# A four-layer sequence kernel: sums issued two pairs late, larger rings, background steps that end their slot, and some norms' statistics on ScalarE

## The chip, the cores and the metric

The kernel runs on one core of a Trainium2 chip. The metric is the device time of one execution in microseconds, given as the median of several runs. All data are float32.

## What is computed

`x` has two batches of 1024 positions with 256 features. Four layers follow each other, each conditioned on a vector of 512 values per batch, and each adds its result to its input.

```python
# layer 0: a selective scan
xn = layernorm(x, g, b) * (1 + scale) + shift          # shift, scale, gate from silu(c)
x_in, z = split(xn @ in_proj)                           # 2 x 512 channels
u = silu(causal_conv4(x_in) + conv_b)
dt_r, B, C = split(u @ x_proj)                          # 64, 16, 16
dt = softplus(dt_r @ dt_proj + dt_b)
h[t] = exp(dt[t] * A) * h[t-1] + (dt[t] * u[t]) * B[t]  # 512 channels x 16 states
y = sum_n(h[t] * C[t]) + u * D
x = x + gate * ((y * silu(z)) @ out_proj)
# layer 1: norm, affine (= skip), norm, then two such scans of one projection, forward and
#          backward in time; both multiplied by silu(mx), added, projected; plus skip
# layer 2: attention with softmax over features (q) and positions (k): k^T v first, then q
# layer 3: ordinary attention, 16 heads of 16, softmax over 1024 positions
```

Layers 2 and 3 end with a norm of the result, an affine, a silu, a projection and the addition to `x`.

## The kernel before

**The scans.** There are six scan passes: layer 0 for batch 0 and 1, then layer 1 forward and backward for batch 0, and the same for batch 1. A pass has 64 tiles of 128 rows by 1024 positions, where the rows are 32 channels by 4 states. Each tile takes five steps. ScalarE makes the decay `dA` in PSUM from `sp0`, the spread `dt` (`decay`, line 133). GpSimd makes the input from `sp1` and the row tile `bc[0]` (`inputs`, line 936). VectorE runs the recurrence (`tile`, lines 943 and 947). The product with `bc[1]` is made on VectorE (line 950), or, for some tiles, on GpSimd (line 949). TensorE adds up the states with the `fold` matrix (`fold`, line 974) into a bank `ys`, after `begin` has put `u * D` there (lines 960 and 964). Four pairs of tiles fill one bank, and `finish` (line 982) multiplies it by the gate and stores it.

**The order.** `chain` writes the order out by hand, pair by pair. Within pair `p` it issues inputs up to tile `2p+4` and decays up to `2p+2`, so that these run ahead. A running figure `lead`, kept from `spent["DVE"]` and the work given to GpSimd, decides which tile's product goes to GpSimd. The sums of pair `p-1` are issued at the end of pair `p`. The tile that an input fills lives until its sums are done; there are 8 such tiles (`hbp`). Decays alternate between two PSUM tiles.

**The work behind the scans.** All other work (norms, projections, conditioning, layers 2 and 3 of batch 0) is written as generators whose steps stand in a queue, `Behind`. Twice a pair, `slot` runs steps as long as there is credit, counted in TensorE columns (`RATES` per slot, at most `2 * T` saved), and room on ScalarE and GpSimd. Each engine executes its instructions in the order written. DMAs are issued from the SP queue, also in order; `later` and `save` put a DMA off by some slots, and `until` forces steps where something must be ready.

**Norms.** `normed` runs `stats` (VectorE, two rows for each 256 columns, lines 394 and 395), `root` (ScalarE, Ln and Exp), `refine` (one Newton step: seven small rows on GpSimd during the scans, lines 410 to 416, else four on VectorE) and `scaled` (eight ScalarE rows, line 133, or VectorE in the last stage). The scan stage holds eight norms.

**Lead-in.** Before the first tile, batch 0 passes through layer 0's norm, affine (`affine`), transposes (`channels`), projection, convolution and `ssm_inputs`. Then the first `sp` and `bc` tiles are loaded.

**Attention.** After the scans, `attention` runs layer 3's scores (line 1418), maxima (1427), exponentials and sums (1458), with layer 2 of batch 1 between them.

## Time and profile before

| | |
|---|---|
| median of 3 runs | 2124.39 us (2119.06 to 2125.03) |
| profiled execution | 2117.43 us, its span 2115.4 us |
| VectorE busy | 1745.5 us, 83% of the span |
| GpSimd busy | 1356.9 us, 64% |
| TensorE busy | 1626.8 us, 77% |
| ScalarE busy | 1140.4 us, 54% |
| DMA queue | 266.07 MB, 37.1% of 16 engines |

In the profile, PE is TensorE, DVE is VectorE, ACT is ScalarE, POOL is GpSimd and SP issues the DMAs. A row of the windows view gives a stretch, its length, the busy time of each engine in it with the number of its instructions, the granted TensorE clock as a share of full speed, the share of the DMA engines' time, and GB/s. A row of the waits view gives who waited for whom, the microseconds in total, the number of times, and the longest. A row of the timeline gives start, duration, engine, line, operation, output and input, and in brackets the idle time before it with what ended it.

### The profile page before, as it was taken

The page shows a single profiled execution, that of the slowest core. Times are in us where ns is not written, and L with a number is a line of the kernel's source. Part 1 is how long each engine was busy: PE and PEld are TensorE (multiplying, and loading weights), DVE is VectorE, ACT ScalarE, POOL GpSimd, SP SyncE. Part 2 cuts the span into 40 slices and gives each one's busy share as a digit, 9 for nine tenths or more (in the row PEclk, how much of TensorE's full clock was granted, in tenths as well). Part 3 has the DMA queues.
Part 4 walks back from the last instruction along what each step waited for, and adds up shares of the span by engine and source line. Part 5 has one row for each costly group of instructions (what it writes and reads, how often), then busy time and mean ns, then how long its engine had stood idle before and what let it go on. Part 6 is the DMA issues. An engine that isn't in the chain of part 4 may idle for free.

```text
span 2115.4 us, 22775 instructions
## 1 busy us (share of the span) xinstructions
PE 1626.8 (77%) x8112; PEld 617.7 (29%) x8112; DVE 1745.5 (83%) x1728; ACT 1140.4 (54%) x1583; POOL 1356.9 (64%) x667
## 2 busy tenths in 40 slices
PE   6576867288697547886945658944999899999997
PEld 3132313033141202222312323300545333333333
DVE  4688898898999999998999987998767757777763
ACT  5565666375546345764555453542044555656665
POOL 0789898898999999999998977998101211000000
PEclk9688968599796558988977865965899999999999
DMA  3663458245653555555653344332300111020001
GB/s 111 239 222 114 157 184 292 83 157 185 254 196 141 179 172 187 189 179 188 250 206 110 117 159 144 123 132 73 116 1 1 39 21 18 23 56 1 2 1 38
DMA packets 106870, 267.53 MB, mean 126 GB/s; under 512 B 14618, under 2 KB 39067, under 8 KB 106756
## 3 DMA queue, kind: packets, MB, share of 16 engines
q1 hardware_dynamic: 106756, 266.07, 37.1%
q8 instruction: 64, 1.05, 0.2%
q14 instruction: 50, 0.41, 0.1%
HBM read 195.90 MB, written 67.90 MB: 125 GB/s over the span
## 4 chain that ended last, share of the span: by engine, by line
PE 30%; DVE 10%; POOL 5%; issue 4%; ACT 2%; DMA 0%; DVEq 0%; ACTq 0%; POOLq 0%
PE sc_t L1418 13%; PE av_t L1458 6%; PE sc_t L95 4%; POOL hb_t L936 3%; PE bank_t L95 3%; DVE dA_t L943 2%; DVE mh L1427 2%; PE sc_t L99 2%; DVE dA_t L947 2%; POOL hb_t L949 1%; PE ys_t L974 1%; DVE hb_t L943 1%; ACT act_t L133 1%; POOL act_t L141 1%; DVE hb_t L947 1%
## 5 line engine op out<-in xcount | busy, mean ns | idle before, releaser
L936 POOL TENSOR_TENSOR hb_t<-sp,bc 128x1024 f32<-128x1024 f32 x384 | 908.8, 2399 | 88.5 <-PE ys_t L974 52.0
L133 ACT ACTIVATE dA_t<-sp,negA 128x1024 f32<-128x1024 f32 x384 | 428.5, 1117 | 548.3 <-DVE hb_t L950 432.8
L947 DVE TENSOR_TENSOR_SCAN dA_t<-dA_t,hb_t 128x1024 f32<-128x1024 f32 x195 | 445.9, 2287 | 62.3 <-ACT dA_t L133 35.1
L1427 DVE TENSOR_REDUCE mh<-sc_t 128x1 f32<-128x512 f32 x512 | 327.5, 686 | 110.2 <-PE sc_t L1418 109.8
L974 PE MATMUL ys_t<-hb_t,fold 128*32 128x512 f32 x1536 | 294.2, 781 | 153.5 <-POOL hb_t L949 101.1
L133 ACT ACTIVATE hb_t<-sc_t 128x512 f32<-128x512 f32 x512 | 276.9, 595 | 188.7 <-PE sc_t L1418 188.5
L950 DVE TENSOR_TENSOR hb_t<-dA_t,bc 128x1024 f32<-128x1024 f32 x285 | 349.1, 1225 | 21.4 <-DVE dA_t L947 0.5
L1418 PE MATMUL sc_t<-act_t 32*128 32x512 f32 x2048 | 336.6, 650 | 11.0 <-DVE mh L1427 7.3
L949 POOL TENSOR_TENSOR hb_t<-hb_t,bc 128x1024 f32<-128x1024 f32 x99 | 235.7, 2381 | 19.6 <-DVE hb_t L947 17.8
L784 POOL TENSOR_TENSOR act_t<-act_t,row 128x1024 f32<-128x1024 f32 x8 | 18.7, 2347 | 339.9 <-PE sc_t L99 193.3
L943 DVE TENSOR_TENSOR_SCAN dA_t<-dA_t,hb_t 128x1024 f32<-128x1024 f32 x90 | 205.7, 2285 | 9.2 <-POOL hb_t L936 6.0
L1458 PE MATMUL av_t<-hb_t,act_t 128*32 128x256 f32 x2048 | 164.3, 393 | 1.1 <-DVE act_t L1466 1.1
L95 PE MATMUL bank_t<-act_t,w_c_w 128*128 128x512 f32 x256 | 129.6, 657 | 41.2 <-ACT act_t L133 41.2
L133 ACT ACTIVATE act_t<-bank_t,cols 128x512 f32<-128x512 f32 (+1 forms) x206 | 129.9, 677 | 44.5 <-PE bank_t L95 38.7
L1418 PEld LDWEIGHTS sc_t<-act_t 32*128 32x128 f32 x2048 | 111.1, 185 | 120.9 <-issue 79.9
L974 PEld LDWEIGHTS ys_t<-hb_t,fold 128*32 128x32 f32 x1536 | 40.5, 123 | 358.9 <-POOL hb_t L949 139.5
L947 DVE TENSOR_TENSOR_SCAN hb_t<-dA_t,hb_t 128x1024 f32<-128x1024 f32 x61 | 139.0, 2279 | 3.9 <-ACT dA_t L133 3.6
L141 POOL TENSOR_TENSOR act_t<-act_t 128x1024 f32<-128x1024 f32 x50 | 118.4, 2367 | 0.2
L99 PE MATMUL bank_t<-ident,act_t 128*128 128x128 f32 x128 | 34.6, 426 | 92.5 <-ACT act_t L133 92.3
L95 PE MATMUL bank_t<-act_t,w_dt_w 64*128 64x512 f32 x96 | 74.6, 912 | 40.4 <-ACT act_t L133 34.4
L1458 PEld LDWEIGHTS av_t<-hb_t,act_t 128*32 128x32 f32 x2048 | 42.1, 108 | 190.5 <-issue 177.8
L1363 POOL MEMSET act_t<- 128x1024 f32 x8 | 7.6, 952 | 128.0 <-PE sc_t L1418 128.0
(176 smaller groups left out, 1833.9 us busy)
## 6 DMA issues: line engine op xcount, KB each, us to landing
sp<-dt SPq DMA_DIRECT2D x192, 512.0 KB, 5.3
dt<-act_t SPq DMA_DIRECT2D x48, 512.0 KB, 5.2
bc<-bc SPq DMA_DIRECT2D x48, 512.0 KB, 7.7
u<-act_t SPq DMA_DIRECT2D x24, 512.0 KB, 5.0
fu<-u SPq DMA_DIRECT2D x24, 512.0 KB, 4.5
y<-y SPq DMA_DIRECT2D x96, 128.0 KB, 5.8
g<-act_t SPq DMA_DIRECT2D x16, 512.0 KB, 5.3
fg<-g SPq DMA_DIRECT2D x64, 128.0 KB, 4.7
```

The source lines that it names most:

```text
L95: nc.tensor.matmul(o, w, x, **kw)
L133: nc.scalar.activation(o, x, func, **kw)
L141: nc.gpsimd.tensor_tensor(o, x, y, op)
L936: nc.gpsimd.tensor_tensor(e, self.sp[c, 1], self.bc[0][k], ALU.mult)
L943: nc.vector.tensor_tensor_scan(h[:, ::-1], dA[:, ::-1], e[:, ::-1], 0.0, ALU.mult, ALU.add)
L947: nc.vector.tensor_tensor_scan(h, dA, e, 0.0, ALU.mult, ALU.add)
L949: return lambda: nc.gpsimd.tensor_tensor(e, h, self.bc[1][k], ALU.mult)
L950: nc.vector.tensor_tensor(e, h, self.bc[1][k], ALU.mult)
L974: nc.tensor.matmul(self.ys[d, cp][at : at + DS, :], fold, e[:, ts(ch, 512)], start=False, stop=(k == NK - 1),)
L1418: nc.tensor.matmul(ps, w[r, ts(at, P)], x[r, ts(wide_at, 512)], start=True, stop=True)
L1427: nc.vector.tensor_reduce(mh[n][:, t, ch, j : j + 1], ps, AX.X, ALU.max)
L1458: nc.tensor.matmul(sums.av[32 * j : 32 * j + 32, ts(part, 256)], sts[b]["v"][t // 2][:, t % 2, 4 * g + j, :], es[j // 2][:, at : at + 256] ...
```

## The change

- The sums of pair `p-2` are issued at the end of pair `p`, and there are 9 input tiles instead of 8.
- `sp0` has four buffers instead of three and is loaded a step earlier. `bc` has a ring of four for each of its two kinds instead of one of eight, and the first kind is loaded ahead of a pair's slots. `u` and `y` for `begin` are loaded in halves, one for each bank.
- A step may yield `REST`: the slot then ends. Roots, refinements and the exponentials of layer 2 do so. The credit cap is `4 * T`, and three rates are higher.
- `refine` is always on VectorE. Statistics are made by `moments` on ScalarE (mean and sum of squares by the accumulator) for the norms that come while `mode["easy"]` is set: layer 1 of batch 1, and layers 2 and 3 of batch 0.
- In the lead-in, half of `scaled`, the affine, half of the transposes' evictions, both copies of `dbl` and the first input run on VectorE, and the first `bc` tile is loaded as soon as it is stored.
- `cond_later` runs once for each batch, the second time before `cond_last`, and loads its weights each time.
- Some small tiles move to other pools.

```diff
-RATES = (2048, 2048, 1250, 1300, 1500, 1500)
+RATES = (2048, 2600, 1500, 1500, 1500, 1500)
...
+REST = -1
...
     act = ctx.enter_context(tc.tile_pool(name="act", bufs=15))
-    hbp = ctx.enter_context(tc.tile_pool(name="hbp", bufs=8))
+    hbp = ctx.enter_context(tc.tile_pool(name="hbp", bufs=9))
...
-    mode = {"bank": "bank", "scans": False, "tail": False, "least": 640}
+    mode = {"bank": "bank", "scans": False, "tail": False, "least": 640, "easy": False}
...
             at = mod[:, scale_at + c, :]
+            if not mode["scans"]:
+                t = small_t((P, B), "aff")
+                nc.vector.tensor_scalar(t, at, 1.0, None, ALU.add)
+                nc.vector.tensor_scalar(s[:, c, :], t, g_c, None, ALU.mult)
+                nc.vector.scalar_tensor_tensor(
+                    o[:, c, :], t, b_c, mod[:, shift_at + c, :], ALU.mult, ALU.add
+                )
+                continue
...
-    def cond_later():
+    def cond_later(b):
...
         nc.sync.dma_start(g1[:, 1, :], a["norm1_b"].partition_broadcast(P))
-        yield 5 * T
+        yield 7 * T
...
         yield from pipe(*(
-            cond_rows(w, scb, brow, i * D, b, f"{name}1_{b}", res)
-            for b in range(B)
-            for i, (name, res) in enumerate(
-                (("shift", made), ("scale", made), ("gate", cond["gate1"]))
-            )
+            cond_rows(w, scb, brow, i * D, b, name, res)
+            for i, (name, res) in enumerate((
+                ("shift1", made), ("scale1", made),
+                ("gate1" if b == 0 else "gate0_0", cond["gate1"]),
+            ))
         ))
...
-    def root(mv):
+    def moments(src, mv):
+        for j in range(0, 4, 2):
+            for k in (j, j + 1):
+                act_f(
+                    small_t((P, 2, D), "t2", 1)[:, 0, :], src[:, k, :], AF.Identity,
+                    scale=-1.0 / D, accum_out=mv[:, k, 0:1],
+                )
+            for k in (j, j + 1):
+                act_f(
+                    small_t((P, 2, D), "t2", 1)[:, 0, :], src[:, k, :], AF.Square,
+                    bias=mv[:, k, 0:1], accum_out=mv[:, k, 1:2],
+                )
+            spent["ACT"] += 4 * 250
+            yield 320
+    def root(mv, easy):
         r = small_t((P, mv.shape[1]), "rstd", 2)
-        act_f(r, mv[:, :, 1], AF.Ln, bias=eps)
+        act_f(r, mv[:, :, 1], AF.Ln, bias=eps, scale=1.0 / D if easy else 1.0)
...
-    def refine(mv, r):
+    def refine(mv, r, easy):
         q = small_t((P, mv.shape[1]), "newt", 2)
-        e = nc.gpsimd if mode["scans"] else nc.vector
-        if mode["scans"]:
-            e.tensor_scalar(q, mv[:, :, 1], EPS, None, ALU.add)
-            e.tensor_tensor(q, q, r, ALU.mult)
-            e.tensor_tensor(q, q, r, ALU.mult)
-            e.tensor_scalar(q, q, -0.5, 1.5, ALU.mult, ALU.add)
-            e.tensor_tensor(r, r, q, ALU.mult)
-            e.tensor_scalar(q, mv[:, :, 0], -1.0, None, ALU.mult)
-            e.tensor_tensor(q, q, r, ALU.mult)
-            spent["POOL"] += 900
-            return q
-        e.scalar_tensor_tensor(q, mv[:, :, 1], EPS, r, ALU.add, ALU.mult)
-        e.scalar_tensor_tensor(q, q, -0.5, r, ALU.mult, ALU.mult)
-        e.scalar_tensor_tensor(r, q, 1.5, r, ALU.add, ALU.mult)
-        e.scalar_tensor_tensor(q, mv[:, :, 0], -1.0, r, ALU.mult, ALU.mult)
+        if easy:
+            nc.vector.tensor_scalar(q, mv[:, :, 1], 1.0 / D, EPS, ALU.mult, ALU.add)
+            nc.vector.tensor_tensor(q, q, r, ALU.mult)
+        else:
+            nc.vector.scalar_tensor_tensor(q, mv[:, :, 1], EPS, r, ALU.add, ALU.mult)
+        nc.vector.scalar_tensor_tensor(q, q, -0.5, r, ALU.mult, ALU.mult)
+        nc.vector.scalar_tensor_tensor(r, q, 1.5, r, ALU.add, ALU.mult)
+        nc.vector.scalar_tensor_tensor(
+            q, mv[:, :, 0], 1.0 if easy else -1.0, r, ALU.mult, ALU.mult
+        )
+        spent["DVE"] += 600
...
-    def scaled(src, r, q):
+    def scaled(src, r, q, i):
         o = abuf((P, 4, D))
-        for j in range(4 if mode["tail"] else 0):
+        far = mode["tail"] or i and not mode["scans"]
+        for j in range(4 if far else 0):
...
             )
-        for j in range(0 if mode["tail"] else 4):
+        for j in range(0 if far else 4):
...
         for i, t in enumerate(src):
-            stats(t, mv[:, ts(i, 4), :])
-            yield
-        r = root(mv)
-        yield mode["least"] * 3 // 2
-        q = refine(mv, r)
-        yield
+            if easy:
+                yield from moments(t, mv[:, ts(i, 4), :])
+            else:
+                stats(t, mv[:, ts(i, 4), :])
+                yield
+        r = root(mv, easy)
+        yield REST
+        q = refine(mv, r, easy)
+        yield REST
         for i, t in enumerate(src):
-            res.append(scaled(t, r[:, ts(i, 4)], q[:, ts(i, 4)]))
+            res.append(scaled(t, r[:, ts(i, 4)], q[:, ts(i, 4)], i))
...
         def take(i, c, ps):
+            if c and not (mode["scans"] or mode["tail"]):
+                nc.vector.tensor_scalar(
+                    dst[c][:, ts(i, 512)], ps, scale(c), bias(c), ALU.mult, ALU.add
+                )
+                return
...
                     )
-            take(0, pss[0])
-            nc.vector.tensor_copy(dbl[:, 512:], pss[1][: R + 2 * N, :])
+            for ch in range(2):
+                nc.vector.tensor_copy(dbl[:, ts(ch, 512)], pss[ch][: R + 2 * N, :])
...
         save(2, st["bc"], dbl[R : R + 2 * N, :])
+        if "first" in st:
+            later(2, st["first"])
...
             yield from normed(xt, skip)
+            yield REST
...
                 nc.vector.tensor_tensor(v, v, twice(cond["s1"][b], 4), ALU.mult)
+                spent["DVE"] += 1800
...
                 yield
+            yield REST
+            yield REST
...
                     least = next(self.queue[0])
+                    if least == REST and not mode["tail"]:
+                        self.credit -= max(work[0] - at, mode["least"])
+                        return 0
...
                 return
-            self.credit = min(self.credit + columns, 2 * T)
+            self.credit = min(self.credit + columns, 4 * T)
...
-        def load_bc(self, k):
-            for w in range(2):
-                t = bcp.tile([P, T], F32, tag="bc", name="bc")
-                at = w * N + k * NS
-                nc.sync.dma_start(
-                    t,
-                    self.st["bc"][at : at + NS, :].unsqueeze(0).to_broadcast([DS, NS, T]),
-                )
-                self.bc[w][k] = t
+        def load_bc(self, k, w):
+            t = bcp.tile([P, T], F32, tag=f"bc{w}", name=f"bc{w}")
+            at = w * N + k * NS
+            nc.sync.dma_start(
+                t, self.st["bc"][at : at + NS, :].unsqueeze(0).to_broadcast([DS, NS, T])
+            )
+            self.bc[w][k] = t
...
             behind.until(lambda: len(self.st["have"]) > c // 4)
-            t = spread.tile([P, T], F32, tag=f"sp{w}", name=f"sp{w}")
+            t = spread.tile([P, T], F32, tag=f"sp{w}", name=f"sp{w}", bufs=4 - w)
...
-        def load_rest(self, d):
+        def load_rest(self, d, cp):
...
                 srcs["y"] = self.add.st["y"]
...
-                t = fin.tile([P, T], F32, tag=f"f{key}", name=f"f{key}")
-                nc.sync.dma_start(t, src[ts(d, P), :])
-                self.rest[d][key] = t
+                rest[key] = t = fin.tile([P, 512], F32, tag=f"f{key}", name=f"f{key}")
+                for ch, half in enumerate(self.halves(src, d, cp)):
+                    nc.sync.dma_start(t[ts(ch, 64), :], half)
...
-        def inputs(self, c, k):
+        def inputs(self, c, k, engine=nc.gpsimd):
             e = hb()
-            nc.gpsimd.tensor_tensor(e, self.sp[c, 1], self.bc[0][k], ALU.mult)
+            engine.tensor_tensor(e, self.sp[c, 1], self.bc[0][k], ALU.mult)
...
         behind.until(lambda: s.st["have"])
-        for w in range(2):
-            s.load_spread(0, w)
-        s.load_bc(0)
-        for w in range(2):
-            s.load_spread(1, w)
+        for c in range(2):
+            for w in range(2):
+                s.load_spread(c, w)
+        s.load_bc(0, 1)
         for k in range(1, NK):
-            s.load_bc(k)
-        s.load_rest(0)
+            for w in range(2):
+                s.load_bc(k, w)
+        s.load_rest(0, 0)
         ahead(0, "decay")
-        ahead(0, "inputs")
+        made["inputs"][0] = s.inputs(0, 0, nc.vector)
...
                     nxt[0].load_spread(nxt[1], w)
-            if k == 2 and cp == 1:
-                if d < 3:
-                    s.load_rest(d + 1)
-                elif nxt:
-                    nxt[0].load_rest(0)
+            if k == 1 and nxt:
+                nxt[0].load_spread(nxt[1] + 1, 0)
+            if final and i + 1 < len(scans):
+                scans[i + 1].load_bc(k, 0)
+            if k == 3 and nxt:
+                nxt[0].load_rest(nxt[1] // 4, nxt[1] // 2 % 2)
...
             ahead(2 * p + 2, "decay")
-            if k == 2 and nxt:
-                nxt[0].load_spread(nxt[1] + 1, 0)
...
             if final and i + 1 < len(scans):
-                scans[i + 1].load_bc(k)
-            if p:
-                fold(p - 1)
-        fold(len(pairs) - 1)
+                scans[i + 1].load_bc(k, 1)
+            if p > 1:
+                fold(p - 2)
+        for p in (2, 1):
+            fold(len(pairs) - p)
...
             nc.vector.tensor_reduce(mx, kT, AX.X, ALU.max, negate=True)
-            yield
+            yield REST
...
             act_f(kT, kT, AF.Exp, bias=mx, accum_out=sm)
-            yield
+            yield REST
...
             nc.vector.reciprocal(sm, sm)
-            yield
+            yield REST
...
             held[0] -= 1
-            yield
+            yield REST
             act_f(q, q, AF.Exp)
-            yield mode["least"] * 3 // 2
+            yield REST
...
-        at = small.tile([P, 2, P], F32, tag="at", name="at", bufs=1)
+        at = small_t((P, 2, D), "t2", 1)[:, :, :P]
...
             if n not in mh:
-                mh[n] = small.tile([P, NT, 2, 4], F32, tag="mh", name="mh", bufs=2)
+                mh[n] = tails.tile([P, NT, 2, 4], F32, tag="mh", name="mh", bufs=2)
...
     ctx.enter_context(tc.manual_schedule())
+    nc.scalar.preload_act_table_set("natural_log_exp_and_others")
...
             s.enter_context(tc.tile_pool(name=n, bufs=k))
-            for n, k in (("bcp", 8), ("spread", 3), ("fin", 1), ("yp", 2))
+            for n, k in (("bcp", 4), ("spread", 3), ("fin", 1), ("yp", 2))
...
         s00 = Scan("00", negA[0], "D0", False, True)
+        s00.st["first"] = lambda: s00.load_bc(0, 0)
...
                     x_of[self.n][self.b].extend(self.res[0])
+                    mode["easy"] = (self.n, self.b) != (1, 0) and not mode["tail"]
...
         behind.add(
-            cond_first(), cond_later(), p01, p10, p20, cond_last(), p11, p21,
+            cond_first(), cond_later(0), p01, p10, p20, cond_later(1), cond_last(), p11, p21,
...
     home[0] = ctx.enter_context(tc.tile_pool(name="act2", bufs=17))
+    tails = ctx.enter_context(tc.tile_pool(name="tails", bufs=1))
     psum.append(ctx.enter_context(tc.tile_pool(name="psA", bufs=1, space=bass.MemoryType.PSUM)))
-    mode.update(scans=False, tail=True, bank="sc")
+    mode.update(scans=False, tail=True, easy=False, bank="sc")
...
```

## The prediction

> **What bounds the kernel now.** I read the page first (spans, then slices), then a windows table cut at the first scan of each of the six scan passes, then who waited for whom inside the scan stage, then the timeline around the longest waits.
>
> ```profile
> span 2115.4 us, 22775 instructions
> PE 1626.8 (77%) x8112; PEld 617.7 (29%) x8112; DVE 1745.5 (83%) x1728; ACT 1140.4 (54%) x1583; POOL 1356.9 (64%) x667
> ...
> DVE  4688898898999999998999987998767757777763
> ...
> POOL 0789898898999999999998977998101211000000
> ```
>
> ```profile
> core 0: us, PE busy (x) PEld busy (x) DVE busy (x) ACT busy (x) POOL busy (x), PEclk, DMA share, GB/s
> 0.00:69.50 69.50, 42.10 (x108) 21.56 (x108) 25.27 (x43) 34.98 (x51) 7.44 (x16) 0.87 0.42 149
> 69.50:311.20 241.70, 175.78 (x548) 60.79 (x548) 210.46 (x136) 159.53 (x196) 223.01 (x108) 0.80 0.50 171
> 311.20:561.80 250.60, 173.74 (x568) 61.08 (x568) 219.97 (x161) 149.95 (x174) 223.47 (x109) 0.83 0.54 184
> 561.80:792.50 230.70, 151.00 (x498) 53.17 (x498) 217.22 (x156) 112.61 (x145) 221.40 (x108) 0.67 0.54 190
> 792.50:1010.30 217.80, 173.94 (x546) 55.34 (x550) 206.85 (x123) 126.13 (x140) 209.21 (x91) 0.87 0.57 191
> 1010.30:1249.90 239.60, 151.70 (x624) 66.53 (x620) 227.79 (x181) 118.46 (x150) 211.32 (x100) 0.79 0.48 168
> 1249.90:1478.20 228.30, 153.51 (x520) 52.10 (x520) 201.02 (x133) 103.36 (x122) 207.45 (x106) 0.68 0.35 118
> 1478.20:2115.40 637.20, 605.04 (x4704) 247.09 (x4704) 436.95 (x804) 335.40 (x605) 53.63 (x33) 0.97 0.10 27
> ```
>
> Lead-in 69.5 us, scans 1408.7, attention 637.2. In the scans VectorE is busy 1283.3 us (the six rows added) and GpSimd 1295.9: both about 92%, ScalarE 55%. The stage ends when the slower of two nearly full engines ends. VectorE's idle time is 125 us, most of it in pass 1 (31), pass 2 (31) and pass 6 (27); in passes 3 to 5 it is 11 to 13 each, which is close to what back-to-back instructions leave. Who ends the idle time:
>
> ```profile
> DVE dA_t L947 <- ACT dA_t L133: 35.1, 18, 4.7
> DVE dA_t L947 <- POOL hb_t L936: 27.1, 12, 13.7
> DVE act_t L791 <- PE bank_t L95: 24.5, 7, 7.9
> DVE st L394 <- POOL act_t L141: 7.0, 3, 4.7
> ...
> POOL hb_t L936 <- PE ys_t L974: 52.0, 20, 12.3
> ...
> POOL hb_t L936 <- DMA bc<-bc: 12.5, 4, 4.4
> ```
>
> The reader is to see that no single wait dominates. Behind several stands one chain, here at its clearest in the timeline: the norm's refinement sits on GpSimd behind whole tiles, ScalarE (in order) stands at the row of `scaled` until it is done, the decay behind it is late, and VectorE idles 4.74 us:
>
> ```profile
> 1108.14 0.20 POOL L416 TENSOR_TENSOR newt<-newt,rstd 128x8 f32<-128x8 f32 x1
> ...
> 1108.37 4.05 ACT L133 ACTIVATE act_t<-act_t,newt,rstd 128x256 f32<-128x256 f32 x8 [4.15 <-POOL newt L416]
> ...
> 1113.53 2.30 DVE L947 TENSOR_TENSOR_SCAN dA_t<-dA_t,hb_t 128x1024 f32<-128x1024 f32 x1 [4.74 <-ACT dA_t L133]
> ```
>
> **Part by part.** *Lead-in.* Half of `scaled`, the affine and half of the transposes' evictions go to VectorE. ScalarE's eight rows take 4.05 us from 14.2, then the affine runs on it from 18.2 to 20.6. Now the affine is six VectorE rows of about 0.2 us from 16.4, so the first eviction starts near 17.6 and the first projection near 20.3 instead of 23.1: -2.8. The first `bc` load is issued before `dt` is stored, so it is off the burst of loads that GpSimd waits for at 67.1; its second input waits for the fourth load of that burst instead of the sixth, about -2.5 (loads are seen landing about 1.2 us apart, 67.1 to 70.9). The first tile starts earlier still, but GpSimd feeds the next ones. Sum -5. A rule bears on the first input, now on VectorE with two SBUF operands: the Trainium skill ("SBUF — State Buffer", the shared port pair) says that such an instruction and a GpSimd one that reads SBUF exclude each other. The trace's half-tile pair L611/L612 took 1.18 and 1.68 us side by side; 1.23 is what a full-tile VectorE product (L950, one operand in PSUM) takes, so there was interference. By the rule the gain loses up to 2.4 us once; by the row about 0.6. I keep -5.
>
> *Work taken off.* Five of the eight norms in the scan stage (second batch's layer 1 twice, layer 2 twice, layer 3) lose 40 pairs of BN rows. Eight such pairs run from 5.80 to 10.19, 0.55 each: VectorE -22.0. The refinement moves to it: 8 norms x 4 rows x 0.20 + 5 = +7.4. The built order has 98 products on GpSimd where there were 99: +1.2. VectorE -13.4. GpSimd loses 8 refinements of 1.95 us (1106.35 to 1108.30), one input and one product: -20. The two were level, so VectorE's -13 counts.
> The 80 new ScalarE rows read 128x256. The nearest row, 588 ns, has two pointer operands, and eight in a row take 0.51 each. The Trainium skill ("ScalarE: Activation LUTs", What ACT_TABLE_LOAD costs) gives 186 ns + 0.833 per element, 93 more per pointer and 93 of overlap: an estimate of 0.31 for the mean and 0.40 for the square. Bounds 28 and 41 us in all; I take 41, the trace's row. The same page's rules for authors speak against the move (multiply and add belong on VectorE). By that rule the statistics would cost: 41 us of ScalarE for 22 of VectorE. But ScalarE waited 432.8 us for VectorE to free its PSUM tiles (`ACT dA_t L133 <- DVE hb_t L950`), and a slot may hold only one four-row step (2 us beside a 1.1 us decay in 3.45 us). Hidden, unless it comes just before a decay: +4 for that. The 24 more `dgD` rows (0.39, together 9.4 us) and a third 1024-column copy lie in the same cover. Table loads stay 58.
>
> *Waits removed, on VectorE.* Refinement behind GpSimd tiles: 4.7 above, 3.6 at 187.5, 2.1 at 410.4, 2.1 at 1254.2: -12. Decays that waited for `sp` at a pass's start (2.4 at 317, 2.2 at 568), now a fourth buffer and a load a step earlier: -4.6. Statistics waiting for GpSimd's products (7.0 and 1.0), now with slots ended between: -6. The residual adds' 24.5: 17.5 of them come after transposes that stood until 1251 for a refinement; I take -8, since the adds still follow their products closely. The other decays, late behind evictions and gates (27 left of 44): -5; the longer `7 * T` wait before the gate weights' use is in it. GpSimd's waits for sums and `bc`: only some reached VectorE, -5. Sum -40.
>
> *Waits added.* A sum is issued one pair (6.9 us) later, behind that pair's background products. Three consumers get tighter. `finish` on VectorE comes 4.7 us after the scan that ends the pair (product 1.23, scan 2.28, product 1.23), and now needs a sum issued at that pair's end, not one pair before. In the trace I compared the end of each pair's sums with the end of the scan at whose pair they are issued: median 2.3 us later, a quarter over 4.9, a tenth over 6.8. So about 8 of 32 gated finishes would wait, by some 2 us less what the sums no longer wait for data (PE waited 101.1 for `POOL hb_t L949`): bounds 0 and 16, I take +8. The 16 ungated ones hold up ScalarE, with room. The ring of 9 tiles spans exactly 2p-4 to 2p+4, so the odd input loses one pair of slack: +4, bounds 0 and 26 (half of the 52.0). With ScalarE's +4, +16.
> DMAs: 103 more, mostly half-tile `fu` and `fy`, at 0.3 to 0.6 us of issue, about 50 us over the stage. Behind them stand the gate and `sp` loads. They are needed two pairs later; nothing is charged, a gain is excluded, a loss is bounded by the 34 us that decays waited for `sp`, of which VectorE saw 4.6. The second copy of the ada weights adds 1.5 MB to 267.53, in pass 3.
> *Attention.* Same instructions in the same order apart from renamed tiles and a few products beside each other: 0, +-3.
>
> Sum: -5 - 13 - 40 + 16 = -42. The profiled execution took 2117.4 (its span and 2.0 around it): 2075. The median of the runs shown is 7.0 above it, so 2082 for the runs.
>
> **Rivals.** *Idle falls everywhere to what passes 3 to 5 show.* Six times 12 is 72 instead of 125: -53, with -13 and -5: -71, 2053. For it: the change addresses a cause in each of passes 1, 2 and 6. Against: pass 1 is filled by GpSimd, whose softplus products stay.
> *Only the work counts.* The removed waits turn into waits for GpSimd, which is as full: -18, 2106. For it: 92% beside 92%. Against: 12 of the waits are ScalarE's alone.
> *Late sums starve VectorE, slower.* The credit cap rises from 2048 to 4096 columns and the rates of passes 2 to 4 rise (2048, 1250, 1300 to 2600, 1500, 1500), while ended slots save credit up. A burst of 2048 more columns is four 512-column products of 0.66, 2.6 us. Lags then pass 4.7 where they now pass 2.1: half of the gated finishes, by about 3.2 us: 16 x 3.2 = 51. GpSimd's 52.0 for sums doubles, half of it seen: 26. -58 + 77 = +19, 2143. It decides from 58 us of such stalls on. For it: PE at clock 0.67 to 0.87 already lags at 1286 (GpSimd waited 12.3 there). Against: sums no longer hold PE up, and PE is at 70% in the stage.
> That the statistics never move is excluded by the built order, which holds the 80 rows.
>
> **How the numbers follow.** 0.3%, 6.4 us, is about what a measurement of this kernel tells from no change. Forecast 0.45, deeper gain 0.16, work only 0.20 (0.07 of it within the bound), late sums 0.19. Faster 0.74, same 0.07, slower 0.19. The forecast's own range is 2057 to 2107, from the bounds of the added waits and half of the removed ones. For 8 in 10: down to 2040 (0.06 left out below) and up to 2135 (0.12 above).
>
> **What would show it.** Right: no POOL `newt` rows; `act_t<-POOL newt` waits gone; the first scan near 64.5; VectorE's idle in the scans near 100 us, BN rows 72; PE `ys_t` waits for `POOL hb_t` near nothing. Wrong: `DVE y <- PE ys_t` (2.0 now) above 20 us, or `POOL hb_t <- PE ys_t` above 80, which is the slower rival; decays late behind the new 128x256 rows; a scan stage of 1390 us with GpSimd full, which is the work-only one.

## The result, and the profile after

The changed kernel takes 2188.95 us (median of 4 runs, 2184.42 to 2191.54), the kernel before 2121.72 (median of 4, 2109.71 to 2125.03). The ratio is 1.0323 with a 95% interval of 1.0289 to 1.0357: slower by 3.2%, where a gain of 42 us was forecast. The profiled execution took 2184.4 us, its span is 2182.6.

The changed kernel's page, its span and busy times:

```profile
span 2182.6 us, 23014 instructions
PE 1598.7 (73%) x8112; PEld 618.9 (28%) x8112; DVE 1798.3 (82%) x1700; ACT 1184.4 (54%) x1753; POOL 1349.0 (62%) x609
```

VectorE has 28 instructions fewer than before and 52.8 us more busy time (1745.5 before). The windows table of the changed kernel, cut at the first scan of each pass as before:

```profile
0.00:65.10 65.10, 41.91 (x108) 21.25 (x108) 31.12 (x57) 29.38 (x37) 5.09 (x15) 0.86 0.44 154
65.10:317.90 252.80, 166.61 (x514) 58.64 (x514) 219.94 (x142) 166.34 (x205) 221.64 (x98) 0.77 0.52 173
317.90:575.20 257.30, 170.18 (x560) 59.75 (x560) 226.35 (x166) 146.19 (x174) 223.47 (x96) 0.80 0.53 180
575.20:810.90 235.70, 145.31 (x540) 56.93 (x538) 223.49 (x128) 120.43 (x182) 219.67 (x96) 0.71 0.53 185
810.90:1038.40 227.50, 168.49 (x540) 54.96 (x544) 212.40 (x127) 138.51 (x179) 212.55 (x92) 0.85 0.57 183
1038.40:1289.90 251.50, 157.37 (x633) 69.57 (x634) 229.92 (x155) 129.58 (x196) 211.49 (x91) 0.77 0.45 154
1289.90:1542.40 252.50, 141.64 (x520) 49.18 (x518) 220.43 (x129) 118.80 (x180) 201.46 (x93) 0.71 0.36 114
1542.40:2182.60 640.20, 607.18 (x4704) 248.65 (x4704) 434.65 (x804) 335.12 (x605) 53.58 (x33) 0.96 0.10 26
```

The lead-in is 4.4 us shorter, the scan stage 68.6 longer (1477.3 for 1408.7), attention 3.0 longer: 67.2, which is the difference of the spans. All six passes are longer. Within the scan stage VectorE's busy time rose by 49.2 (the six rows: 1332.5 for 1283.3) and its idle time by 19.4. So most of the loss is not waiting. VectorE's groups in the scan stage (line, shapes, count | busy us, mean ns | idle before) say what it is:

```profile
L433 DVE TENSOR_SCALAR newt<-mv 128x8 f32<-128x8 f32 x5 | 39.8, 7952 | 0.0
L778 DVE TENSOR_TENSOR act_t<-act_t,scale 128x1024 f32<-128x1024 f32 x4 | 10.8, 2692 | 0.0
L436 DVE SCALAR_TENSOR_TENSOR newt<-mv,rstd 128x8 f32<-128x8 f32 x3 | 10.7, 3550 | 0.0
L402 DVE BATCH_NORM_STATS2 st<-act_t 128x6 f32<-128x256 f32 x24 | 9.5, 398 | 2.5 <-DMA act_t<-in_x 2.5
L437 DVE SCALAR_TENSOR_TENSOR newt<-newt,rstd 128x8 f32<-128x8 f32 x8 | 3.4, 428 | 0.3
L438 DVE SCALAR_TENSOR_TENSOR rstd<-newt,rstd 128x8 f32<-128x8 f32 x8 | 3.4, 428 | 0.3
L434 DVE TENSOR_TENSOR newt<-newt,rstd 128x8 f32<-128x8 f32 x5 | 2.9, 589 | 0.5
L439 DVE SCALAR_TENSOR_TENSOR newt<-mv,rstd 128x8 f32<-128x8 f32 x8 | 1.3, 167 | 0.3
```

A row of 128x8 numbers takes 7952 ns on average in one of these lines. The 37 refinement rows take 61.5 us together, where 7.4 were forecast; nine of them are longer than 0.6 us and carry 56.9. The timeline shows the longest, beside GpSimd:

```profile
765.50 1.23 DVE L991 TENSOR_TENSOR hb_t<-dA_t,bc 128x1024 f32<-128x1024 f32 x1
766.64 14.70 DVE L433 TENSOR_SCALAR newt<-mv 128x8 f32<-128x8 f32 x1
769.50 2.54 POOL L990 TENSOR_TENSOR hb_t<-hb_t,bc 128x1024 f32<-128x1024 f32 x1
771.79 9.51 POOL L977 TENSOR_TENSOR hb_t<-sp,bc 128x1024 f32<-128x1024 f32 x4
781.44 0.17 DVE L434 TENSOR_TENSOR newt<-newt,rstd 128x8 f32<-128x8 f32 x1
781.64 0.17 DVE L437 SCALAR_TENSOR_TENSOR newt<-newt,rstd 128x8 f32<-128x8 f32 x1
```

The row ends at 781.34; the last of GpSimd's seven rows beside it ended at 781.31. After that GpSimd pauses and the next small rows take 0.17 each. All nine long rows end 22 to 31 ns after the end of a GpSimd row. VectorE's scans and products go on beside GpSimd at 2.29 and 1.23 us as before. Those have one operand, `dA`, in PSUM; the refinement rows have all operands in SBUF.

The second thing in the profile is the waits of the scan stage (us, times, longest), against those shown of before:

```profile
POOL hb_t L977 <- PE ys_t L1015: 107.7, 30, 15.3
...
DVE y L1023 <- PE ys_t L1015: 24.3, 6, 10.4
DVE dA_t L988 <- ACT dA_t L135: 23.8, 15, 4.1
...
DVE dA_t L988 <- POOL hb_t L977: 20.7, 20, 3.0
...
DVE act_t L827 <- PE bank_t L97: 11.2, 7, 3.3
```

In the kernel before, `finish` had one wait, at the end of the stage:

```profile
DVE y L982 <- PE ys_t L974: 2.0, 1, 2.0
```

The waits that the change was to shorten did shrink: residual adds 24.5 to 11.2, decays on that line 35.1 to 23.8. New are five waits of `finish` for TensorE besides that last one, 24.3 us where it was 2.0, and GpSimd's wait for the sums is twice what it was (52.0). All five waits of `finish` stand behind background projections (`L97`) on TensorE. The longest of both kinds have one cause:

```profile
1381.76 2.08 PE L97 MATMUL bank_t<-w_vo_w,act_t 128*128 128x256 f32 x4
...
1391.21 2.08 PE L97 MATMUL bank_t<-w_vo_w,act_t 128*128 128x256 f32 x4
1393.22 1.22 PE L97 MATMUL bank_t<-row,ones 1*128 1x256 f32 x2
1394.36 1.94 PE L1015 MATMUL ys_t<-hb_t,fold 128*32 128x512 f32 x8
1396.39 0.69 DVE L1023 TENSOR_TENSOR y<-ys_t,fg 128x512 f32<-128x512 f32 x1 [10.44 <-PE ys_t L1015]
1396.40 2.39 POOL L977 TENSOR_TENSOR hb_t<-sp,bc 128x1024 f32<-128x1024 f32 x1 [15.34 <-PE ys_t L1015]
```

The last tile product of the sums was ready at 1381 (GpSimd, 1378.70 for 2.35 us), but the sums were issued a pair later, behind four sets of projections on TensorE's queue. VectorE stood at the gate product and GpSimd had no free input buffer.

### The profile page after: what moved, and what is told of

Read it like the earlier page. It is cut to its first block, busy times and chain, and to the rows that moved or that the text cites. A ratio compares the mean times of both kernels' runs of the same rounds, so it can differ in the third digit from the quotient of the medians.

```text
span 2182.6 us, 23014 instructions
## 1 busy us (share of the span) xinstructions
PE 1598.7 (73%) x8112; PEld 618.9 (28%) x8112; DVE 1798.3 (82%) x1700; ACT 1184.4 (54%) x1753; POOL 1349.0 (62%) x609
## 5 line engine op out<-in xcount | busy, mean ns | idle before, releaser
L977 POOL TENSOR_TENSOR hb_t<-sp,bc 128x1024 f32<-128x1024 f32 x383 | 915.7, 2426 | 151.7 <-PE ys_t L1015 107.7
L988 DVE TENSOR_TENSOR_SCAN dA_t<-dA_t,hb_t 128x1024 f32<-128x1024 f32 x194 | 443.7, 2287 | 44.8 <-ACT dA_t L135 23.8
L1015 PE MATMUL ys_t<-hb_t,fold 128*32 128x512 f32 x1536 | 269.7, 733 | 171.1 <-POOL hb_t L990 131.6
L984 DVE TENSOR_TENSOR_SCAN dA_t<-dA_t,hb_t 128x1024 f32<-128x1024 f32 x92 | 210.4, 2287 | 19.2 <-POOL hb_t L977 14.2
L97 PE MATMUL bank_t<-act_t,w_c_w 128*128 128x512 f32 x256 | 125.3, 641 | 29.0 <-ACT act_t L135 29.0
L97 PE MATMUL bank_t<-act_t,w_dt_w 64*128 64x512 f32 x96 | 70.3, 858 | 55.1 <-ACT act_t L135 47.6
L97 PE MATMUL bank_t<-act_t 128*128 128x256 f32 (+5 forms) x160 | 60.6, 540 | 42.4 <-DMA act_t<-in_ada_w 29.8
```

The lines of the kernel that those rows point to most:

```text
L97: nc.tensor.matmul(o, w, x, **kw)
L977: engine.tensor_tensor(e, self.sp[c, 1], self.bc[0][k], ALU.mult)
L984: nc.vector.tensor_tensor_scan(h[:, ::-1], dA[:, ::-1], e[:, ::-1], 0.0, ALU.mult, ALU.add)
L988: nc.vector.tensor_tensor_scan(h, dA, e, 0.0, ALU.mult, ALU.add)
L1015: nc.tensor.matmul(self.ys[d, cp][at : at + DS, :], fold, e[:, ts(ch, 512)], start=False, stop=(k == NK - 1),)
```

## The experiments

Times are medians; where no other kernel is named, differences are to the changed kernel's 2188.95. A ratio is always to the kernel before, with its 95% interval. The kernel before had 2121 to 2122 in every comparison. The first four runs put the two suspects side by side.

**The refinement back on GpSimd** (`a_pool`).

```
+    if mode["scans"]:
+        e = nc.gpsimd
...
+        e.tensor_tensor(q, q, r, ALU.mult)
+        e.tensor_tensor(q, q, r, ALU.mult)
+        e.tensor_scalar(q, q, -0.5, 1.5, ALU.mult, ALU.add)
+        e.tensor_tensor(r, r, q, ALU.mult)
...
+        return q
```

> The changed kernel with the refinement of the norms in the scans put back on GpSimd (seven small steps; the easy norms' first step takes 1/D as a factor, their last needs no sign). Theory A (the small refinement rows on VectorE take microseconds because GpSimd, which works back to back, keeps VectorE from SBUF; 61 us of such rows where 7 were forecast): about 58 us come back, 2125 to 2140 us, VectorE's busy time falls by 55 to 60 us and the waits of GpSimd for PE's sums fall from 108 us to about 55. Rival B (the sums two pairs late, their inputs and the finish steps that wait for PE, cost the time): within 10 us of the changed kernel, 2180 to 2200. Rival C (statistics and other later steps bunch up on ScalarE): the same as B, or some us slower since GpSimd gets 9 us of work more.

Measured: 2154.58, ratio 1.0150 (1.0130 to 1.0169). VectorE's busy time fell by 59.8 as theory A said (1738.5), but only 34 us came back, and GpSimd's wait for sums didn't fall to 55: it is 116.1. A second cost stood behind the first.

**One row less, and no `tensor_scalar`** (`a_stt`).

```
-    nc.vector.tensor_scalar(q, mv[:, :, 1], 1.0 / D, EPS, ALU.mult, ALU.add)
-    nc.vector.tensor_tensor(q, q, r, ALU.mult)
+    nc.vector.scalar_tensor_tensor(q, mv[:, :, 1], D * EPS, r, ALU.add, ALU.mult)
+    nc.vector.scalar_tensor_tensor(q, q, -0.5 / D, r, ALU.mult, ALU.mult)
...
```

> The changed kernel with the easy norms' first two refinement steps (a tensor_scalar of 128x8 and a product) written as one scalar_tensor_tensor with D*EPS added and 1/D moved into the next step's factor: one row less in each of five refinements, and no tensor_scalar among them. Theory A in the form that the tensor_scalar alone is what GpSimd keeps out (39.8 us in 5 rows): 30 to 40 us come back, about 2152. Theory A in the form that whichever small row comes first waits for GpSimd: under 10 us, since the scalar_tensor_tensor then takes the 8 us in its place. Rivals B and C: under 3 us.

Measured: 2190.97, no change. The small rows still take 59.3 us, the longest 13.82. It isn't the one operation: the row put in its place was held instead (13.82), and where a first row came through, the next ones stood (three of 2.3 us from 166 on).

**The sums one pair late again** (`a_early`).

```
-    if p > 1:
-        fold(p - 2)
+    if p:
+        fold(p - 1)
...
```

> The changed kernel with each pair's sums issued one pair late, as before the change, and the input ring left at nine. Theory A: within 12 us of the changed kernel either way (what the small rows cost VectorE stays). Rival B (the sums' lateness is what cost the time: inputs waiting for PE 108 us, finish steps 23 us): 40 to 70 us come back, 2120 to 2150, with the finish steps' waits for PE back at about 2 us.

Measured: 2163.09, ratio 1.0198 (1.0179 to 1.0216). 26 us came back, less than rival B said and more than theory A. `finish` waits only at the end of the stage again (2.0), and GpSimd's line `L977 <- PE ys_t` is down to 28.8. The small rows still take 49.6.

**The kernel before, with only the refinement moved** (`b_dve`).

```
-    e = nc.gpsimd if mode["scans"] else nc.vector
-    if mode["scans"]:
+    e = nc.vector
+    if False:
...
+    if mode["scans"]:
+        spent["DVE"] += 600
```

> The kernel before with one edit: the refinement of the norms in the scans goes to VectorE in four scalar_tensor_tensor rows each, none of the rest of the change. Theory A in the form that any small row on VectorE between GpSimd's is held: seven to eight refinements of four rows cost VectorE 15 to 40 us where GpSimd gets 9 us back, 2125 to 2150 us. Theory A in the form that only tensor_scalar is held (8 us each; scalar_tensor_tensor rows about 0.8 us on average): 2110 to 2128, no difference. Rivals B and C: 2110 to 2121, slightly faster since the chain of seven steps on GpSimd is gone.

Measured: 2158.61, ratio 1.0171 (1.0153 to 1.0190): this part of the change alone costs 37 us, more than the 2125 to 2150 that theory A gave. (The running figures move along, so GpSimd has 102 products for 99.) VectorE's groups of it in the scan stage:

```profile
L419 DVE SCALAR_TENSOR_TENSOR newt<-mv,rstd 128x8 f32<-128x8 f32 x8 | 28.7, 3587 | 2.9 <-ACT rstd L133 2.9
L420 DVE SCALAR_TENSOR_TENSOR newt<-newt,rstd 128x8 f32<-128x8 f32 x8 | 5.7, 713 | 0.3
L421 DVE SCALAR_TENSOR_TENSOR rstd<-newt,rstd 128x8 f32<-128x8 f32 x8 | 5.6, 705 | 0.3
L422 DVE SCALAR_TENSOR_TENSOR newt<-mv,rstd 128x8 f32<-128x8 f32 x8 | 5.6, 696 | 0.3
```

That is 45.6 us for 32 rows. The idle before them is small; the time is inside the rows, so no table of waits shows it. The kernel before has the same four lines on VectorE in its lead-in and its attention stage, where GpSimd has little to do. There, in its own trace, two of them read:

```profile
L419 DVE SCALAR_TENSOR_TENSOR newt<-mv,rstd 128x8 f32<-128x8 f32 x4 | 1.2, 298 | 3.2 <-ACT rstd L133 3.2
L420 DVE SCALAR_TENSOR_TENSOR newt<-newt,rstd 128x8 f32<-128x8 f32 x4 | 0.7, 166 | 0.1
```

The mean of 298 hides one row, the only one of the four `L419` that met a row of GpSimd:

```profile
1646.39 2.85 POOL L1364 TENSOR_SCALAR act_t<-act_t,cols 128x1024 f32<-128x1024 f32 x1
1646.81 0.71 DVE L419 SCALAR_TENSOR_TENSOR newt<-mv,rstd 128x8 f32<-128x8 f32 x1
...
1647.56 0.17 DVE L420 SCALAR_TENSOR_TENSOR newt<-newt,rstd 128x8 f32<-128x8 f32 x1
1647.76 0.17 DVE L421 SCALAR_TENSOR_TENSOR rstd<-newt,rstd 128x8 f32<-128x8 f32 x1
```

The sign was there in the trace of before. It also shows a limit of the hold: this `tensor_scalar` of GpSimd held the first row for 0.5 us only, and the next rows, with two operands in SBUF as well, ran inside it.

**Operands in PSUM** (`a_psum`). What holds the rows was still an inference from ends that coincide. This run leaves the refinement on VectorE, in the 32 rows of `a_stt`, and moves one operand; each refinement gets a copy out of PSUM.

```
-    r = small_t((P, mv.shape[1]), "rstd", 2)
+    if mode["scans"]:
+        r = bank()[:, : mv.shape[1]]
+        held[0] += 1
+    else:
+        r = small_t((P, mv.shape[1]), "rstd", 2)
...
+        nc.vector.tensor_copy(o, r)
...
```

> The changed kernel with its refinement still on VectorE, but with rstd in a PSUM bank, so that no row of it reads two operands from SBUF (or reads and writes SBUF with one operand); a copy out of PSUM is added to each refinement. If what holds the rows is that VectorE and GpSimd share a way to SBUF which a row of VectorE needs for its second SBUF operand: every row takes its 0.15 to 0.3 us (about 8 us for all, where the changed kernel has 61), and the time is that of the kernel with the refinement on GpSimd, 2145 to 2160 us. If any small row on VectorE waits for GpSimd: no change, about 2189. If the borrowed bank delays the projections, some 5 to 10 us more than the first figure.

Measured: 2142.86, ratio 1.0096 (1.0059 to 1.0133). The 32 arithmetic rows take 5.2 us, none over 0.17, and the eight copies 1.3. The timeline at the place of the 14.70 us row, in `a_psum`:

```profile
755.65 4.75 POOL L986 TENSOR_TENSOR hb_t<-sp,bc 128x1024 f32<-128x1024 f32 x2
...
758.49 0.16 DVE L437 SCALAR_TENSOR_TENSOR newt<-mv,bank_t 128x8 f32<-128x8 f32 x1
758.69 0.16 DVE L438 SCALAR_TENSOR_TENSOR newt<-newt,bank_t 128x8 f32<-128x8 f32 x1
758.88 0.17 DVE L442 SCALAR_TENSOR_TENSOR bank_t<-newt,bank_t 128x8 f32<-128x8 f32 x1
...
760.37 2.33 POOL L999 TENSOR_TENSOR hb_t<-hb_t,bc 128x1024 f32<-128x1024 f32 x1
```

GpSimd's second input row runs until 760.40 and VectorE's rows pass inside it. Against `a_stt` (2190.97), which has the same arithmetic rows, the operand's place with the bank and the copies that come with it gives 48 us. It gives 46 against the changed kernel, 12 more than `a_pool`, which puts 10.6 us of rows back on GpSimd. Rows that still have all operands in SBUF are still held: the product with `scale` takes 16.8 us for four in this run, up to 7.03, where its four rows took 6.0 before.

**Both costs taken out** (`pe`: `a_pool` with `a_early`).

> The changed kernel with both edits that gave time back alone: the refinement on GpSimd (-34 us alone) and the sums one pair late (-26 us alone). If the two costs are separate, they add: 2189 - 60 = 2129 us. If they share a part (the late sums keep GpSimd's ring full and GpSimd then runs back to back over a small row of VectorE), 2140. In either case nothing is left over the kernel before but a few us, so that the other parts of the change (statistics on ScalarE, rates, rests, lead-in) would sum to between 0 and +20 us.

Measured: 2113.52, ratio 0.9948 (0.9929 to 0.9966): 0.5% under the kernel before, and better than either sum that was expected. The two edits gave 34 and 26 alone and 75 together, so the sum of the two alone leaves 15 out. The lateness costs 26 us where the refinement rows are held and 41 where they aren't. GpSimd's line for sums in `pe` has 11.5 us. What is left of the change is a gain of about 8. But the hold is not gone from `pe`. A row that the change did not touch, which makes layer 2's mask, takes in its scan stage:

```profile
L1194 DVE TENSOR_SCALAR act_t<-act_t 128x1024 f32<-128x1024 int32 x1 | 15.7, 15683 | 0.0
```

It stands beside seven GpSimd rows; in the kernel before it took 1.18. The four products with `scale` take 17.5. Together these five rows have 33.2 us, where they had 7.1 in the kernel before. So the gain of 8 is what is left with 26 us of other rows held.

**What the other parts do.** Three kernels stand on `pe`. `pe_noeasy` leaves the statistics on VectorE.

```
-    mode["easy"] = (self.n, self.b) != (1, 0) and not mode["tail"]
+    mode["easy"] = False
```

> The same kernel with the statistics of every norm left on VectorE (no moments on ScalarE), refinement on GpSimd, sums one pair late. If the statistics on ScalarE gain what was forecast of them (22 us of VectorE's rows), this is 10 to 22 us slower than the kernel with them. Rival C (16 rows and their read-outs, 6.5 us a norm half, keep ScalarE from the decays): equal or up to 15 us faster.

Measured: 2126.87, ratio 1.0026 (1.0012 to 1.0040), 13.4 slower than `pe`. The statistics on ScalarE are a gain, as forecast (the five other rows take 28.3 us here, so the hold is not the reason). `pe_rates` has the old rates and cap.

```
-RATES = (2048, 2600, 1500, 1500, 1500, 1500)
+RATES = (2048, 2048, 1250, 1300, 1500, 1500)
-    self.credit = min(self.credit + columns, 4 * T)
+    self.credit = min(self.credit + columns, 2 * T)
```

> The same kernel (statistics on ScalarE, refinement on GpSimd, sums one pair late) with the rates of before (2048, 2048, 1250, 1300, 1500, 1500) and the credit capped at 2048 columns again. If the higher rates bunch other steps in front of the scans, this is 5 to 15 us faster; if steps now end early enough to spare waits at the turn of a pass, 5 to 10 us slower; no opinion between the theories on the refinement.

Measured: 2112.75, no difference to `pe`. `pe_all` takes both of these, and lets REST steps count as ordinary ones.

```
-    if least == REST and not mode["tail"]:
+    if least == REST:
+        least = None
+    if False:
         self.credit -= max(work[0] - at, mode["least"])
         return 0
```

> The kernel with refinement on GpSimd, sums one pair late, statistics on VectorE, the rates and credit of before, and no step that ends its slot: of the change are left the shorter lead-in, the input ring of nine, the loads of u and y in halves and the longer ring of dt rows. The lead-in's 5 to 6 us should be all of it and a ring of nine gives up to 4: 2111 to 2117 us where the kernel before takes 2121. If it is above 2125, what is left of the change costs time as well.

Measured: 2105.51, ratio 0.9893 (0.9855 to 0.9932), more than the 4 to 10 that the lead-in and the ring were to give.

`pe_easy_norest` is `pe_all` with the statistics on ScalarE again.

> The fastest so far (2105.5 us: refinement on GpSimd, sums one pair late, rates and credit of before, no step that ends its slot) with the norms' statistics on ScalarE added again. The statistics gave 13 us where they were added to the kernel with rests: if that holds here, 2090 to 2097. If the rests are what makes room for them (ScalarE's rows bunch up without rests), 2105 or above.

Measured: 2095.64, ratio 0.9871 (0.9838 to 0.9905), the fastest version, 26 us under the kernel before. It lies in the range expected from the statistics, but in part by luck: it is 9.9 us faster than `pe_all`, and the mask's row, which nobody aimed at, is 7.7 us shorter (0.67 for 8.38). It differs from `pe_rates` only in the steps that end their slot: these cost 17 us there. The five other rows take 19.7 us in `pe_rates` and 7.8 here, so some 12 us more of held rows stand beside these 17. `p_norest` asks the same where the sums are late (`a_pool` without the rests).

> The changed kernel with the refinement on GpSimd, sums two pairs late, and the steps that end their slot as ordinary steps again. With the sums one pair late and the rates of before, taking the rests out gave 17 us (2112.8 to 2095.6). If the rests cost the same here: 2154.6 - 17 = 2138. If they help where rows come from a crowded ring (they part ScalarE's and VectorE's rows of a norm), 2155 to 2165.

Measured: 2157.15, 2.6 over `a_pool`. With late sums, and with the refinement on GpSimd, the rests cost nothing, so nothing here makes them a part of the slowdown. Why they cost 17 us once sums are early wasn't settled: the held rows may be most of it, and that pair also has the rates and the cap of before, where this one has the new ones.

`pe_psum_easy_norest` is the fastest version with the refinement on VectorE and `rstd` in PSUM.

> The fastest so far (2095.6 us: sums one pair late, statistics on ScalarE, rates and credit of before, no rests) with the refinement on VectorE and rstd in a PSUM bank instead of on GpSimd. GpSimd is freed of 10.5 us and VectorE gets 6.6 us; the chain of a norm gets shorter by some 3 us each time. If the move is a gain once no row is held: 2085 to 2093. If the borrowed bank takes it back: 2095 to 2105.

Measured: 2112.37, ratio 0.9939 (0.9919 to 0.9960), 17 us slower than with the refinement on GpSimd and outside both ranges. No refinement row is held, but the mask's row is. It reads here, and then in the fastest version (scan stages):

```profile
L1188 DVE TENSOR_SCALAR act_t<-act_t 128x1024 f32<-128x1024 int32 x1 | 14.7, 14728 | 0.0
```

```profile
L1196 DVE TENSOR_SCALAR act_t<-act_t 128x1024 f32<-128x1024 int32 x1 | 0.7, 667 | 0.0
```

VectorE's busy time in the scan stage is 19.0 us longer than in the fastest version: 14.1 in this row, 6.5 in the refinement, 3.4 in the products with `scale`, less 5 elsewhere. Each first row of a refinement also comes to VectorE before ScalarE's root is done (15.5 us of waits, where GpSimd waited 5.3 at that place), but VectorE's idle time as a whole is shorter (112.2 for 123.4). So the run doesn't say what the move is worth: it changed where another row met GpSimd.

**Where the late sums cost.** Three kernels stand on `a_pool`. `p_fin` puts `finish` one pair later.

```
-    ended = pairs[p - 3][:3] if p > 2 and k == 2 else None
+    ended = pairs[p - 4][:3] if p > 3 and k == 3 else None
```

> The changed kernel with the refinement on GpSimd and the sums two pairs late, and each bank's finish step one pair later (fourth pair of the next bank, where it was the third). With the sums one pair late instead, this kernel had 2113.5 us, so the late sums cost 41 us. If VectorE standing at the finish step (21.5 us of waits for PE) is what costs: those waits go to under 3 us and 15 to 25 us come back, about 2134. If it is the input ring (GpSimd's 116 us of waits for PE's sums): under 8 us, about 2150.

Measured: 2146.42, ratio 1.0101 (1.0045 to 1.0157); its four runs spread from 2129 to 2153, and the interval overlaps that of `a_pool`. The waits at `finish` are gone from the trace but for the last. The profiled execution is the fastest of the four (2129.22), and in it GpSimd's waits for sums are down to 76.8 as well, so what the finish step costs by itself isn't settled. `p_r10` has a ring of ten.

```
-    hbp = ctx.enter_context(tc.tile_pool(name="hbp", bufs=9))
+    hbp = ctx.enter_context(tc.tile_pool(name="hbp", bufs=10))
-    t = spread.tile([P, T], F32, tag=f"sp{w}", name=f"sp{w}", bufs=4 - w)
+    t = spread.tile([P, T], F32, tag=f"sp{w}", name=f"sp{w}", bufs=3)
...
```

The load of `sp0` also goes back to its place of before, and the attention stage has one buffer less.

> The changed kernel with the refinement on GpSimd, the sums two pairs late and an input ring of ten (the ring of sp0 is three again to make room, and one buffer less serves the attention stage, whose time is read apart). Ten buffers give sums that are two pairs late the same room that eight gave sums one pair late. If the ring is what the late sums cost: GpSimd's waits for PE's sums fall from 116 to about 50 us, the scan stage from 1441 to 1415 to 1425. If the finish step is what costs: the scan stage stays at 1433 or more, with VectorE's waits at the finish above 15 us.

Measured: 2131.77, ratio 1.0039 (1.0016 to 1.0063): 23 us came back, scan stage 1426.3 in the profiled execution (its slowest run, 2138.05). GpSimd's waits fell to 76.2, not 50; those at `finish` stayed (22.4). `p_r10_fin` has both.

> The changed kernel with the refinement on GpSimd, the sums two pairs late, the input ring of ten and the finish step one pair later: both remedies of the late sums. If ring and finish are all that the late sums cost, the scan stage is that of the kernel with the sums one pair late, 1408 us (2113 to 2118 us in all, with a few us lost to the attention stage's buffer), VectorE's waits at the finish are under 3 us and GpSimd's waits for PE's sums under 40. If the two remedies give back the same waits, 1423, as each alone gave.

Measured: 2135.66, ratio 1.0079 (1.0044 to 1.0115): no better than the ring alone by the medians, whose intervals overlap. (Its trace, of the fastest of seven runs, has a scan stage of 1414.4, but it can't be set against the slowest run of `p_r10`.) Of the 41 us that the late sums cost, the edit with the ring gave 23 back. GpSimd still waits 65.7 for sums in `p_r10_fin`, against 11.5 with the sums one pair late, so ten buffers did not give back what two pairs of lateness take. Of the 18 us between `p_r10` and `pe`, about 5 lie in the attention stage (644.8 for 640.1), which has a buffer less; the rest is not explained.

## Why the prediction was wrong

*The step that failed* is the term "The refinement moves to it: 8 norms x 4 rows x 0.20 + 5 = +7.4" (meant are 32 and 5 rows of 0.20; as written it gives 11.4). It measured 61.5. The scan stage was to shrink by 37 us and grew by 69, and these rows are 54 of the 106 between. The duration came from rows in the lead-in and the attention stage, where GpSimd is nearly idle (7.4 of 69.5 us, 53.6 of 637.2), and was used in a stage where it is 92% busy; the one row of 0.71 there that did meet GpSimd was passed over. The prediction had the rule at hand: it weighed the shared port pair (the Trainium skill, "SBUF — State Buffer", section "SBUF: two separate sides") for one first input and not for 37 rows that keep their operands in SBUF. The page says that a VectorE instruction with two SBUF inputs and a GpSimd one that reads SBUF, or a VectorE one in a two-port mode and any GpSimd one, exclude each other for the whole instruction. For GpSimd's products of two tiles the trace agrees: long rows end with a GpSimd row, and `a_psum` takes the hold away. In two points the measurement differs. A row lost not to one instruction of GpSimd but to up to seven in a row. And GpSimd's `tensor_scalar` of 2.85 us let the held row finish after 1.13 us, and three more rows with two SBUF operands ran inside it. By the rule alone, an estimate with one GpSimd row of 2.4 us for each of 8 first rows comes to about 20 us; 61.5 was measured.

*Late sums.* The added waits were put at +16: `finish` +8, ring +4, ScalarE +4. `finish` measured +22.3, past the bound of 16, and the lateness as a whole 26 to 41 us by `a_early` and `pe`. About eight waits of 1 us were expected at `finish`; five came, of up to 10.4. VectorE waited 34.9 us for GpSimd's inputs, where it was 19.8 (without the wait before the first scan); it is 41.7 in `a_pool` and 14.2 in `pe`, which differ in the lateness alone. Both signs named for the slower rival are there: `DVE y <- PE ys_t` above 20 and `POOL hb_t <- PE ys_t` above 80, doubled to 107.7 as its text said. But the rival was to win alone, at 2143, as -58 + 77; `a_pool`, which has the late sums and not the held refinement rows, has 2154.6, as -8 + 41 (from `pe`). So late sums did starve VectorE, but both of the rival's sizes were too large, and the held rows were not in it. The lags from the trace of before, median 2.3 us with a tenth over 6.8, were charged by their middle; the waits came from the tail, whose longest here is a queue of projections 13 us long (1381.76 to 1394.36).

*Waits removed.* The -40 was not had either. VectorE's idle time in the scans, 125 us, was to fall to about 100. It is 144.8 in the changed kernel, and without the waits at `finish` it fell by 3 us. In `pe`, which has no late sums and no held refinement, it is 116.0. Its waits for decays, all lines together, were 44.2 before, 34.1 in the changed kernel and 49.3 in `pe`: what was freed at one place was waited for at another. That fits the rival "Only the work counts", but no run tested it.

*What held.* Lead-in -5: -4.4. BN rows -22.0: -23.4. Products on GpSimd 98 for 99. Attention 0 +-3: +3.0, at the bound. Of the single waits to be removed, the residual adds gave 13.3 where 8 was taken, the waits for `newt` on GpSimd are gone, and so are the statistics' waits for GpSimd's products (7.0; a wait of 2.5 for a load came). ScalarE's statistics took 51.6 us, not 41, because each of the 80 rows is followed by a read-out. The kernel before has four such read-outs of 0.19 each; the prediction did not count them:

```profile
L135 ACT ACTIVATE t<-act_t,mv 128x256 f32<-128x256 f32 x40 | 20.3, 508 | 1.3
L135 ACT ACTIVATE t<-act_t 128x256 f32<-128x256 f32 x40 | 16.3, 409 | 0.6
L135 ACT ACTIVATION_READ_ACCUMULATOR t<-act_t,mv 128x1 f32 x40 | 7.5, 187 | 0.0
L135 ACT ACTIVATION_READ_ACCUMULATOR t<-act_t 128x1 f32 x40 | 7.5, 187 | 0.0
```

It was hidden all the same; the move gave 13.4 net in `pe`, so the rule weighed against it (multiply and add belong on VectorE; the Trainium skill, "ScalarE: Activation LUTs", Rules for kernel authors) did not decide with VectorE this full. The rows, 0.41 and 0.51, lie above the page's estimate of 0.31 and 0.40, which took off 93 ns for rows that overlap; a read-out stands between these, and without the 93 the estimate from the page is 0.40 and 0.49. "GpSimd -20" came to -5.6 of busy time (1290.3 for 1295.9): the refinement rows that left were busy for 11.9, where the prediction counted 15.6 with the gaps between them, and the 383 input rows became 27 ns longer each, about 10 us.

*The gain.* Work, waits and lead-in were to give 58 us (13, 40 and 5). `pe`, without held refinement rows and late sums, gives 8, and `pe_easy_norest`, without rests and with the rates of before, 26. Between them the five other rows fall from 33.2 to 7.8 us. So no run reached half of that gain; the rests, counted as a help for the statistics' waits, cost 17 us between `pe_rates` and `pe_easy_norest`.

## What to carry to other kernels

A duration read in a stage where another engine is idle doesn't hold where that engine is full: before a small step is moved to VectorE, look at where its operands lie and at what GpSimd does at that moment. An operand in PSUM, or the step left on the busy engine, is then cheaper than a row that looks like 0.2 us. Look afterwards at every group whose mean has grown, and not only at what was moved: here a row that no edit touched went from 1.18 to 15.68 us. When a consumer is made later, count what else is issued on that queue in between, since here it was the longest such burst, not the median lag, that stopped the engines on both sides.

## What the runs showed of the hardware that was not expected

- A VectorE row of 128x8 with its operands in SBUF took 0.17 us beside an idle GpSimd and up to 14.70 beside a busy one, through seven GpSimd rows. In the scan stages of four kernels, all 39 such rows over 0.6 us ended 21 to 31 ns after a GpSimd row. With `rstd` in PSUM, 40 rows took 0.15 to 0.17.
- The hold takes a one-operand `tensor_scalar` from SBUF to SBUF as well as `scalar_tensor_tensor`: changing the form moved the hold to the row in its place and gained nothing. The mask's `tensor_scalar` of 128x1024 took 0.67 in `pe_easy_norest` and 15.68 in `pe`, through seven GpSimd rows.
- What GpSimd runs matters. Its products of two tiles held the rows to their end; its `tensor_scalar` of 2.85 us let a held row end 1.13 us into it, and three more ran inside it at 0.17, in the kernel before as in the changed one; beside a `memset` of 0.95 us four rows with two operands in SBUF ran at 0.17, but the one-operand `tensor_scalar` in front of them (11.95 us) stood to the end of one.
- The held time is booked as busy time of the row, with no idle time before it.
